# The feed-forward's last down products, moved into the first two steps of the attention that follows

## The chip, the cores and the metric

The kernel runs on one core of one Trainium2 chip. The metric is the device time of one execution in microseconds, the median over several runs. A profiled execution is a separate one; its durations are used to cost single steps, and its own total is given beside its span. The engines are named as in the profile: PE (TensorE matmuls), PEld (its weight loads), DVE (VectorE), ACT (ScalarE), POOL (GpSimd), SP (the engine that issues most DMAs).

## The reference

Input is x, 4096 tokens (16 sequences of 256) of 256 values, all in float32. Four parts follow one another, each with a residual sum and a layer norm:

```python
x = layernorm(x + L0_attn(x))   # a linear recurrence with decay, 16 heads of 128
x = layernorm(x + L0_ffn(x))    # silu(x Wg) * (x Wu) @ Wd, hidden size 704, weights stored as integers
x = layernorm(x + L1_attn(x))   # latent attention: 16 heads, causal, 256 keys per sequence
x = layernorm(x + L1_ffn(x))    # 32 experts, 4 per token, and two shared experts
```

The second one, `down(silu(gate) * up)`, and the third matter here. In the third, a token's query goes through a latent of 192 values and its keys and values through one of 64, each with an RMS norm:

```python
cq  = rms_norm(x @ w_qa.T)                  # 192
ckv = x @ w_kva.T                           # 64 latent + 64 rotary
q   = cq @ w_qb.T                           # 16 heads of 128 + 64 rotary
k, v = (rms_norm(ckv[:64]) @ w_kvb.T)       # per head 128 and 128
out = softmax(mask(q k.T * scale)) @ v @ w_o.T
```

The kernel does not form k and v: it multiplies w_qb with w_kvb's key half, and w_kvb's value half with w_o, once (the "products" below, tiles w_q, w_qr and w_ov), and then scores and sums over the 64-value latent itself.

## The kernel before

Tokens are taken in 8 blocks of 512 (`NB`), each of four tiles of 128 tokens (`NTT`); x lies in SBUF throughout (`xs`, of which `x_t` are the tiles).

**The feed-forward** (from about 860 us) is a loop over blocks, `for b in range(NB)`. A block has five chunks of gate and up matmuls over 512 tokens (`glu`, line 211; silu on ACT, line 219; the product on DVE, line 221) and a half chunk (`glu_rest`, lines 229 to 243). Both write the gated values `hT`, from a pool with two buffers. Then comes the next block's transposed x (line 182), and then the previous block's down products: `finish_ffn(b, hT)` runs two pairs of token tiles (`down`, lines 250 and 256; ten matmuls of 128x256 and two of 64x256 in each pair) into two PSUM tiles `d_ps`, and `added` adds them to x on DVE (line 192) and takes the layer norm: statistics on DVE (153, 154), a scalar step on DVE (144), a power on POOL (145), the normalising step on DVE (169). After the loop the last block's `finish_ffn` is called once more; nothing else of the feed-forward is left then.

In blocks 2 and 3 the loop also runs `products(0)` and `products(1)`, each for eight heads (matmuls at 816 and 829, copies at 823 on DVE and 836 on ACT). Their weights come in two halves `wqb` and `wo1` in one buffer each (DMAs at 781 and 783), so that the second half waits for the last reader of the first; `wkvb` is loaded whole (762). Blocks 4 to 7 run the latents of the second attention's block 0 in pieces (`latents`).

**The second attention** (to about 1907 us) runs 64 steps of one pair of heads over one block, with an order written out by hand under `tc.manual_schedule`: each engine executes its instructions in the order of the code. The loop is `for n in range(-2, NS + 1)`. Step n does three things for different pairs: it asks for the queries of pair n + 2 (`queries`, PE lines 1075 and 1081, two PSUM tiles from a pool of three; `turn`, the rotary part, three DVE operations at 1090 to 1092 and an addition on POOL at 1093), scores pair n + 1 (`scores`, PE 1111, two PSUM buffers; `maxima`, DVE 1122; `exps`, ACT 1135; `divide`, a reciprocal on DVE at 1146 and a product on POOL at 1148), and forms the contexts of pair n - 1 (`keys_first`, transposes on PE 1161 and a copy `aT` on ACT 1165; `contexts`, PE 1174; the copy into `cT` on ACT 1336). Steps -2 and -1 have no contexts yet, and step 0 neither.

Between these come, piece by piece, the latents of the next block: `latents(1)` runs in the first steps. It has a transposed x, four latent tiles (PE 687, copy 694 and squares 697 on ACT), the RMS scale (DVE 144, POOL 145), eight scaled copies `cq` on ACT (711, 712), the key side `kf` on DVE (720 to 732), and transposes (739, 746). Three latent tiles are taken in step -2 and the fourth in step -1. In the code of one step the order is:

```python
heads[0].scores / maxima / exps         # pair n+1, first head
sms[n][1].divide()                      # second head of pair n
q_ps = queries(...)                     # pair n+2
heads[0].divide()
aTs0 = keys_first(pair, 0)              # pair n-1
qTs[asked] = [turn(...) ...]
heads[1].scores(...); contexts(...); keys_first(pair, 1)
heads[1].maxima(...); second_place(...) # latents, outputs, routing
heads[1].exps(...); contexts(...)
```

After it come the experts. Their weights `w_e` are loaded by 26 DMAs that SP issues from about 1870 us on, as their space, which the second attention's tiles hold, comes free; the first expert product is at 1993.44 us.

## Time and profile before

| | |
|---|---|
| time, median of 3 runs | 2123.05 us (2122.95 to 2123.97) |
| profiled execution | 2142.67 us, of which the span is 2140.9 us |
| mean granted TensorE clock in it | 0.991 |
| PE busy | 2056.8 us, 96% of the span |
| DVE, ACT, POOL busy | 1567.0 (73%), 754.8 (35%), 878.3 us (41%) |
| first attention | to about 860 us |
| feed-forward | about 860 to 1124 us |
| second attention | about 1112 to 1907 us |
| first expert product | 1993.44 us |

The profiled execution took 19.6 us more than the median of the runs; rows of the profile are read against its own total. A row of the timeline has the start in the span, the busy time, the engine, the line, the operation with its output and inputs, and in brackets the idle time of the engine just before it and what released it. The share of busy time is a mean over the four stages, so a stage is read by its own stretch.

### The profile page before, as it was taken

The page shows a single profiled execution, that of the slowest core. Times are in us where ns is not written, and L with a number is a line of the kernel's source. Part 1 is how long each engine was busy: PE and PEld are TensorE (multiplying, and loading weights), DVE is VectorE, ACT ScalarE, POOL GpSimd, SP SyncE. Part 2 cuts the span into 40 slices and gives each one's busy share as a digit, 9 for nine tenths or more (in the row PEclk, how much of TensorE's full clock was granted, in tenths as well). Part 3 has the DMA queues.
Part 4 walks back from the last instruction along what each step waited for, and adds up shares of the span by engine and source line. Part 5 has one row for each costly group of instructions (what it writes and reads, how often), then busy time and mean ns, then how long its engine had stood idle before and what let it go on. Part 6 is the DMA issues. An engine that isn't in the chain of part 4 may idle for free.

```text
span 2140.9 us, 29447 instructions
## 1 busy us (share of the span) xinstructions
PE 2056.8 (96%) x9496; PEld 1434.1 (67%) x9496; DVE 1567.0 (73%) x4000; ACT 754.8 (35%) x2213; POOL 878.3 (41%) x948
## 2 busy tenths in 40 slices
PE   8999999999999999999998999999999999988897
PEld 5777777777777777556565666666666666664675
DVE  7888888888888887232327669797988879873556
ACT  2212121212111211211315566656565665541233
POOL 5622232323232322000005554667575767653357
PEclk9999999999999999999999999999999999999999
DMA  9544444444444220300000000000000000050438
GB/s 310 188 133 148 133 140 133 138 128 138 134 143 121 90 89 29 90 16 20 1 1 1 1 1 1 24 9 6 3 4 2 3 3 3 10 186 2 137 131 321
DMA packets 101402, 169.73 MB, mean 79 GB/s; under 512 B 17527, under 2 KB 66431, under 8 KB 99072
## 3 DMA queue, kind: packets, MB, share of 16 engines
q1 hardware_dynamic: 88512, 158.45, 23.3%
q0 software_dynamic: 8064, 5.18, 0.8%
q10 hardware_dynamic: 4672, 4.21, 0.6%
q8 instruction: 76, 1.25, 0.2%
q14 instruction: 78, 0.64, 0.1%
HBM read 128.76 MB, written 56.95 MB: 87 GB/s over the span
## 4 chain that ended last, share of the span: by engine, by line
PE 75%; DVE 16%; ACT 3%; issue 3%; DMA 1%; POOL 1%; another core or an unknown queue 1%; POOLq 0%; DVEq 0%; SPq 0%; ACTq 0%
PE p_ps L422 16%; PE o_ps L515 10%; PE v_ps L452 9%; PE s_ps L1111 5%; PE g_ps L211 4%; PE u_ps L211 4%; PE o_ps L1193 4%; PE d_ps L250 3%; PE q_ps L1075 3%; PE c_ps L1174 3%; PE a_ps L1161 3%; DVE sm L1122 2%; PE q_ps L1081 2%; DVE turned L1092 2%; DVE turned L1091 1%
## 5 line engine op out<-in xcount | busy, mean ns | idle before, releaser
L502 POOL TENSOR_TENSOR wkv<-su,Wr_sb 128x512 f32<-128x512 f32 x128 | 160.2, 1273 | 503.2 <-PE p_ps L422 313.9
L1148 POOL TENSOR_TENSOR pr<-pr,rr 128x256 f32<-128x256 f32 (+1 forms) x256 | 206.9, 836 | 153.3 <-DVE rr L1146 126.0
L515 PE MATMUL o_ps<-w_o,wkv 128*128 128x256 f32 (+1 forms) x1024 | 251.6, 388 | 6.1 <-POOL wkv L502 5.8
L1135 ACT ACTIVATE pr<-sm,nm 128x128 f32<-128x128 f32 (+1 forms) x512 | 226.2, 444 | 78.9 <-DVE nm L1122 64.7
L452 PE MATMUL v_ps<-xm,w_Wv 128*128 128x512 f32 x512 | 242.4, 596 | 6.5 <-DMA w_Wv<-in_Wv_dram 6.5
L515 PEld LDWEIGHTS o_ps<-w_o,wkv 128*128 128x128 f32 x1024 | 192.1, 190 | 75.7 <-POOL wkv L502 44.9
L1111 PE MATMUL s_ps<-kT,qT 128*128 128x128 f32 (+1 forms) x1024 | 198.0, 337 | 23.6 <-DVE nm L1122 23.6
L424 ACT COPY t_sb<-p_ps 128x256 f32<-128x256 f32 x128 | 47.4, 370 | 467.1 <-PE p_ps L422 465.7
L422 PE MATMUL p_ps<-xm,w_Wk 128*128 128x256 f32 x896 | 204.3, 379 | 1.5 <-DVE Wr_sb L427 1.5
L422 PEld LDWEIGHTS p_ps<-xm,w_Wk 128*128 128x128 f32 x896 | 170.4, 190 | 52.7 <-issue 27.8
L422 PE MATMUL p_ps<-xm,w_Wr 128*128 128x256 f32 x896 | 204.4, 379 | 0.7 <-POOL xm L404 0.5
L1093 POOL TENSOR_TENSOR qT<-qT,turned 128x512 f32<-128x512 f32 x128 | 162.8, 1274 | 87.7 <-DVE turned L1092 86.5
L422 PEld LDWEIGHTS p_ps<-xm,w_Wr 128*128 128x128 f32 x896 | 170.0, 190 | 25.2 <-DVE Wk_sb L427 0.9
L1111 PEld LDWEIGHTS s_ps<-kT,qT 128*128 128x128 f32 x1024 | 146.0, 193 | 44.5 <-issue 36.9
L1165 ACT COPY aT<-a_ps 128x384 f32<-128x384 f32 x256 | 109.9, 480 | 167.3 <-PE a_ps L1161 167.2
L473 DVE TENSOR_TENSOR_SCAN st<-decay,kv 128x255 f32<-128x255 f32 x256 | 163.8, 681 | 4.4
L1122 DVE CUSTOM_DVE_ANT_0 sm<-s_ps,const 128x128 f32<-128x128 f32 (+1 forms) x512 | 154.1, 353 | 14.5 <-PE s_ps L1111 11.5
L1007 POOL DMA_INDIRECT xp_d<-xs,dest x128 | 128.3, 1003 | 59.5 <-issue 30.9
L497 ACT ACTIVATE Wr_sb<-Wr_sb 128x512 f32<-128x512 f32 x128 | 73.5, 621 | 217.7 <-DVE Wr_sb L430 188.7
L145 POOL TENSOR_TENSOR rstd<-rs_t,nhalf 128x4 f32<-128x4 f32 (+1 forms) x33 | 33.3, 1010 | 285.0 <-DVE rs_t L144 274.5
L452 PEld LDWEIGHTS v_ps<-xm,w_Wv 128*128 128x128 f32 x512 | 97.7, 191 | 74.8 <-issue 61.8
L221 DVE TENSOR_TENSOR hT<-sg,u_ps 128x512 f32<-128x512 f32 x56 | 38.4, 686 | 139.7 <-PE u_ps L211 131.4
(190 smaller groups left out, 3711.4 us busy)
## 6 DMA issues: line engine op xcount, KB each, us to landing
w_Wk<-wsum_d SPq DMA_DIRECT2D x56, 448.0 KB
w_Wr<-wsum_d SPq DMA_DIRECT2D x56, 448.0 KB
w_Wv<-in_Wv_dram SPq DMA_DIRECT2D x64, 256.0 KB
res_d<-zeros SPq DMA_DIRECT2D x16, 1024.0 KB
res<-res_d SPq DMA_DIRECT2D x16, 1024.0 KB
w_e<-in_W_experts_dram SPq DMA_DIRECT2D x32, 384.0 KB
xp_d<-empty SPq DMA_DIRECT2D x4, 1360.0 KB
xe<-xp_d SPq DMA_DIRECT2D x32, 136.0 KB
```

The source lines that it names most:

```text
L211: mm = nc.tensor.matmul(ps, lhsT=w[:, c, i * P : (i + 1) * P], rhs=xT[:, c, :], start=(c == 0), stop=(c == DC - 1),)
L422: nc.tensor.matmul(to, lhsT=w[:, at, :], rhs=x[:, bt, :], start=True, stop=True)
L452: nc.tensor.matmul(ps, lhsT=self.w3["Wv"][:, 2 * h + c, :], rhs=self.xms["Wv"][:, 2 * c : 2 * c + 2, :].rearrange("p s t -> p (s t)"), sta ...
L473: nc.vector.tensor_tensor_scan(st[:, s, 1:], decay[:, n : n + 1].to_broadcast([P, S - 1]), kv[:, s, : S - 1], 0.0, ALU.mult, ALU.add,)
L502: nc.gpsimd.tensor_tensor(wkv, self.su[h], self.both(self.r, h), ALU.mult)
L515: nc.tensor.matmul(ps.rearrange("p t d -> p (t d)") if opens else ps[:, tt % 2, :], lhsT=self.wkv[h][:, tt * P : (tt + 1) * P], rhs=w_o[:, ...
L1007: put = nc.gpsimd.indirect_dma_start(out=xp_d[:, :], out_offset=bass.IndirectOffsetOnAxis(ap=dest[:, k, t : t + 1], axis=0), in_=xs[b][:, ...
L1093: nc.gpsimd.tensor_tensor(qT, qT, qr, ALU.add)
L1111: nc.tensor.matmul(ps[:, lo:hi], lhsT=qT[:, s * S + i * P : s * S + (i + 1) * P], rhs=kT[:, s * S : s * S + hi - lo], start=True, stop=True,)
L1122: nc.vector.tensor_tensor_reduce(out=sm[:, lo:hi], in0=self.ps[s][:, lo:hi], in1=cst["mask"][:, lo:hi], scale=-(DQ**-0.5), scalar=-MASKED, ...
L1135: nc.scalar.activation(self.pr[:, s, lo:hi], self.sm[s][:, lo:hi], AF.Exp, bias=self.nm[:, s, i : i + 1], scale=-1.0, accum_out=self.rs[:, ...
L1148: nc.gpsimd.tensor_tensor(self.pr[:, :, lo:hi], self.pr[:, :, lo:hi], rr[:, :, i : i + 1].to_broadcast([P, 2, hi - lo]), ALU.mult,)
```

## The change

The last block's down products leave the end of the feed-forward. Their two pairs become a generator, `downs`; the attention's loop takes one pair in step -1 and one in step 0, just after the queries. Their PSUM tiles stand, until step 1, in the two banks that later hold the transposed probabilities. The adds to x stand in step 0 and the layer norm in step 2.

For this, the last block's gated values and w_down have to live on into the attention. The gated values of odd blocks are written into `ctx_h`, the space of the contexts `cT`, which has two buffers as before; even blocks have a buffer of their own. w_down gets a pool `wd` apart from the other weights, closed at step 1, and the copies `aT` then get a pool that opens at step 1. To make room, the weights for the products come in quarters (`wqb`, `wo1` and now also `wkvb`, four heads each) and `products(0)` to `products(3)` run in blocks 1 to 4.

```diff
-    def glu(xT, wg, wu, chunks, pool, psum, tag, more=0):
-        hT = pool.tile([P, chunks + more, BLK], F32, tag="hT", name="hT")
+    def glu(xT, wg, wu, chunks, pool, psum, tag, hT=None):
+        if hT is None:
+            hT = pool.tile([P, chunks, BLK], F32, tag="hT", name="hT")
...
+    pc = att.enter_context(tc.tile_pool(name="ctx", bufs=1, reuse_waits="tile"))
+    ctx_h = pc.tile([P, 2, NH // 4, BLK], F32, name="ctx_h")
...
+    def load_quarter(part):
+        rows = slice(part * QH * P, (part + 1) * QH * P)
+        wqb = wt.tile([P, QH, QLR], F32, tag="wqb", name="wqb")
+        nc.sync.dma_start(out=wqb, in_=a["w_qb_nope"][rows, :].rearrange("(h p) j -> p h j", p=P))
+        wo1 = wt.tile([P, QH, D], F32, tag="wo1", name="wo1")
+        nc.sync.dma_start(out=wo1, in_=a["w_o"][rows, :].rearrange("(h p) d -> p h d", p=P))
+        wkvb = wt.tile([P, QH, 2, KVLR], F32, tag="wkvb", name="wkvb")
+        rows = slice(2 * rows.start, 2 * rows.stop)
         nc.sync.dma_start(
+            out=wkvb, in_=a["w_kvb"][rows, :].rearrange("(h x p) c -> p h x c", x=2, p=P)
         )
+        return wqb, wo1, wkvb
+    quarters = [load_quarter(part) for part in range(4)]
+    def down_pairs(two, hT):
+        os = []
+        for pair in range(NTT // 2):
+            pss = [ps[:, pair, :] for ps in two]
+            down(pss, hT, w_down, 2 * pair)
+            os += pss
+            yield os
...
+        hT2 = [
+            ph_.tile([P, NF + 1, BLK], F32, name="hT", bufs=1),
+            ctx_h.rearrange("p i j t -> p (i j) t")[:, : NF + 1, :],
+        ]
...
+            hT = glu(xT, w_gate, w_up, NF, ph_, ps_g, "g", hT2[b % 2])
...
-                if b in (NB - 6, NB - 5):
-                    products(b - NB + 6)
-            finish_ffn(*last)
+            if NB - 7 <= b <= NB - 4:
+                products(b - NB + 7)
...
+        psd = ExitStack()
+        ps_d = psd.enter_context(tc.tile_pool(name="ps_d2", bufs=2, space=PSUM))
+        two = [ps_d.tile([P, 2, D], F32, tag="d", name="d_ps") for _ in range(2)]
+        downs = down_pairs(two, last[1])
...
+                if n == 1:
+                    psd.close()
+                    ffd.close()
+                    ps_a = ph.enter_context(tc.tile_pool(name="ps_a", bufs=2, space=PSUM))
+                    ps_c = ph.enter_context(tc.tile_pool(name="ps_c", bufs=1, space=PSUM))
+                    pt = ph.enter_context(tc.tile_pool(name="att_t", bufs=4))
...
+                if n in (-1, 0):
+                    os = next(downs)
                 if scored is not None:
                     heads[0].divide()
...
-                        cT = cTs[seen // NP, part] = pc.tile(
-                            [P, NP // 2, BLK], F32, tag="cT", name="cT"
-                        )
+                        cT = cTs[seen // NP, part] = ctx_h[:, part]
...
+                if n == 0:
+                    x = x_t[(NB - 1) * NTT :]
+                    for o, y in zip(os, x):
+                        nc.vector.tensor_tensor(y, o, y, ALU.add)
+                if n == 2:
+                    layernorm(x_t[(NB - 1) * NTT :], x_t[(NB - 1) * NTT :])
```

More of the change, by code (lines that the diff above doesn't have):

```diff
@@ L193, in added @@
         layernorm(x, x)
-    ffw = ExitStack()
+    ffd, ffw = ExitStack(), ExitStack()
+    wd = ffd.enter_context(tc.tile_pool(name="wd", bufs=1, side="right"))
+    w_down = wd.tile([P, NF + 1, D], F32, name="w_down")
     wf = ffw.enter_context(tc.tile_pool(name="wf", bufs=1, side="right"))
@@ L200, in seq_postln_kernel @@
     w_gu = wf.tile([P, DC, 2 * HALF], F32, name="w_gu")
-    w_down = wf.tile([P, NF + 1, D], F32, name="w_down")
-    def glu(xT, wg, wu, chunks, pool, psum, tag, more=0):
-        hT = pool.tile([P, chunks + more, BLK], F32, tag="hT", name="hT")
+    def glu(xT, wg, wu, chunks, pool, psum, tag, hT=None):
+        if hT is None:
+            hT = pool.tile([P, chunks, BLK], F32, tag="hT", name="hT")
         for i in range(chunks):
@@ L749, in latents @@
         yield
-    with ExitStack() as ph:
-        wt = ph.enter_context(tc.tile_pool(name="wt", bufs=1, reuse_waits="tile"))
+    pc = att.enter_context(tc.tile_pool(name="ctx", bufs=1, reuse_waits="tile"))
+    ctx_h = pc.tile([P, 2, NH // 4, BLK], F32, name="ctx_h")
+    wts = ExitStack()
+    wt = wts.enter_context(tc.tile_pool(name="wt", bufs=1, reuse_waits="tile"))
+    nc.sync.dma_start(
+        out=w_lat[:, :, :QLR], in_=a["w_qa"].rearrange("(c p) o -> p c o", p=P)
+    )
+    nc.sync.dma_start(
+        out=w_lat[:, :, QLR:], in_=a["w_kva"].rearrange("(c p) o -> p c o", p=P)
+    )
@@ new lines, in seq_postln_kernel @@
+    nc.sync.dma_start(out=q_ln, in_=a["q_a_ln_w"])
+    nc.sync.dma_start(out=kv_ln, in_=a["kv_a_ln_w"].partition_broadcast(P))
+    w_pe = a["w_qb_pe"].rearrange("p (h k d) -> p h k d", k=2, d=DR)
+    nc.sync.dma_start(
+        out=w_q[:, :, KVLR:], in_=a["w_qb_pe"][:P, :].rearrange("p (h d) -> p h d", h=NH)
+    )
+    for k in range(2):
+        nc.sync.dma_start(out=w_qr[k * QR : (k + 1) * QR, :, KVLR:], in_=w_pe[P:, :, k, :])
+    nc.sync.dma_start(
+        out=w_router, in_=a["router_w"].rearrange("(c p) e -> p c e", p=P)
+    )
@@ new lines, in seq_postln_kernel @@
+    nc.sync.dma_start(out=e_bias, in_=a["e_bias"].partition_broadcast(P))
+    for w, n in ((sh_gate, "shared_gate"), (sh_up, "shared_up"), (sh_down, "shared_down")):
+        nc.sync.dma_start(out=w, in_=a[n].rearrange("(c p) o -> p c o", p=P))
+    QH = NH // 4
+    def load_quarter(part):
[6 more added lines that the diff above has]
+        rows = slice(2 * rows.start, 2 * rows.stop)
@@ L753, in seq_postln_kernel @@
         nc.sync.dma_start(
-            out=w_lat[:, :, :QLR], in_=a["w_qa"].rearrange("(c p) o -> p c o", p=P)
+            out=wkvb, in_=a["w_kvb"][rows, :].rearrange("(h x p) c -> p h x c", x=2, p=P)
         )
-        nc.sync.dma_start(
-            out=w_lat[:, :, QLR:], in_=a["w_kva"].rearrange("(c p) o -> p c o", p=P)
-        )
-        nc.sync.dma_start(out=q_ln, in_=a["q_a_ln_w"])
-        nc.sync.dma_start(out=kv_ln, in_=a["kv_a_ln_w"].partition_broadcast(P))
-        wkvb = wt.tile([P, NH, 2, KVLR], F32, name="wkvb")
@@ L762, in seq_postln_kernel @@
-        nc.sync.dma_start(
-            out=wkvb, in_=a["w_kvb"].rearrange("(h x p) c -> p h x c", x=2, p=P)
-        )
-        w_pe = a["w_qb_pe"].rearrange("p (h k d) -> p h k d", k=2, d=DR)
-        nc.sync.dma_start(
-            out=w_q[:, :, KVLR:], in_=a["w_qb_pe"][:P, :].rearrange("p (h d) -> p h d", h=NH)
-        )
-        for k in range(2):
-            nc.sync.dma_start(out=w_qr[k * QR : (k + 1) * QR, :, KVLR:], in_=w_pe[P:, :, k, :])
-        nc.sync.dma_start(
-            out=w_router, in_=a["router_w"].rearrange("(c p) e -> p c e", p=P)
-        )
@@ L774, in seq_postln_kernel @@
-        nc.sync.dma_start(out=e_bias, in_=a["e_bias"].partition_broadcast(P))
-        for w, n in ((sh_gate, "shared_gate"), (sh_up, "shared_up"), (sh_down, "shared_down")):
-            nc.sync.dma_start(out=w, in_=a[n].rearrange("(c p) o -> p c o", p=P))
-        halves = []
-        for h in (0, NH // 2):
-            rows = slice(h * P, (h + NH // 2) * P)
-            wqb = wt.tile([P, NH // 2, QLR], F32, tag="wqb", name="wqb")
-            nc.sync.dma_start(out=wqb, in_=a["w_qb_nope"][rows, :].rearrange("(h p) j -> p h j", p=P))
-            wo1 = wt.tile([P, NH // 2, D], F32, tag="wo1", name="wo1")
-            nc.sync.dma_start(out=wo1, in_=a["w_o"][rows, :].rearrange("(h p) d -> p h d", p=P))
-            halves.append((wqb, wo1))
@@ L787, in seq_postln_kernel @@
-        with ExitStack() as ff:
-            ph_ = ff.enter_context(tc.tile_pool(name="h1", bufs=2, reuse_waits="tile"))
-            ps_t = ff.enter_context(tc.tile_pool(name="ps_t", bufs=2, space=PSUM))
-            ps_g = ff.enter_context(tc.tile_pool(name="ps_g", bufs=4, space=PSUM))
-            ps_d = ff.enter_context(tc.tile_pool(name="ps_d", bufs=2, space=PSUM))
-            def finish_ffn(b, hT):
-                os = []
-                two = [ps_d.tile([P, 2, D], F32, tag="d", name="d_ps") for _ in range(2)]
-                for pair in range(NTT // 2):
-                    pss = [ps[:, pair, :] for ps in two]
-                    down(pss, hT, w_down, 2 * pair)
-                    os += pss
-                added(b, os)
-            def products(part):
-                wqb, wo1 = halves[part]
-                pairs = range(part * NH // 4, (part + 1) * NH // 4)
-                for pair in pairs:
-                    ps3 = ps_t.tile([P, BLK], F32, tag="t", name="wq_ps")[:, : 3 * KVLR].rearrange(
-                        "p (k d) -> p k d", k=3
-                    )
-                    ps, ps_r = ps3[:, :2, :], ps3[:, 2, :]
-                    for k in range(2):
-                        h = 2 * pair + k
-                        for to, lo, n in ((ps[:, k, :], 0, P), (ps_r[k * QR : (k + 1) * QR, :], P, QR)):
-                            nc.tensor.matmul(
-                                to,
-                                lhsT=wqb[:, h - part * NH // 2, lo : lo + n],
-                                rhs=wkvb[:, h, 0, :],
-                                start=True,
-                                stop=True,
-                            )
-                    nc.vector.tensor_copy(w_q[:, 2 * pair : 2 * pair + 2, :KVLR], ps)
-                    nc.vector.tensor_copy(w_qr[:, pair, :KVLR], ps_r)
-                for pair in pairs:
-                    ps = ps_t.tile([P, BLK], F32, tag="t", name="wo_ps")[:, :D]
-                    for k in range(2):
-                        h = 2 * pair + k
@@ new lines, in load_quarter, with finish_ffn, products @@
+        return wqb, wo1, wkvb
[7 more added lines that the diff above has]
+            yield os
+    with ExitStack() as ff:
+        ph_ = ff.enter_context(tc.tile_pool(name="h1", bufs=2, reuse_waits="tile", side="right"))
+        hT2 = [
+            ph_.tile([P, NF + 1, BLK], F32, name="hT", bufs=1),
+            ctx_h.rearrange("p i j t -> p (i j) t")[:, : NF + 1, :],
+        ]
+        ps_t = ff.enter_context(tc.tile_pool(name="ps_t", bufs=2, space=PSUM))
+        ps_g = ff.enter_context(tc.tile_pool(name="ps_g", bufs=4, space=PSUM))
+        ps_d = ff.enter_context(tc.tile_pool(name="ps_d", bufs=2, space=PSUM))
+        def finish_ffn(b, hT):
+            two = [ps_d.tile([P, 2, D], F32, tag="d", name="d_ps") for _ in range(2)]
+            for os in down_pairs(two, hT):
+                pass
+            added(b, os)
+        def products(part):
+            wqb, wo1, wkvb = quarters[part]
+            pairs = range(part * QH // 2, (part + 1) * QH // 2)
+            for pair in pairs:
+                ps3 = ps_t.tile([P, BLK], F32, tag="t", name="wq_ps")[:, : 3 * KVLR].rearrange(
+                    "p (k d) -> p k d", k=3
+                )
+                ps, ps_r = ps3[:, :2, :], ps3[:, 2, :]
+                for k in range(2):
+                    h = 2 * pair + k
+                    for to, lo, n in ((ps[:, k, :], 0, P), (ps_r[k * QR : (k + 1) * QR, :], P, QR)):
@@ L829, in products @@
                         nc.tensor.matmul(
-                            ps[k * KVLR : (k + 1) * KVLR, :],
-                            lhsT=wkvb[:, h, 1, :],
-                            rhs=wo1[:, h - part * NH // 2, :],
+                            to,
+                            lhsT=wqb[:, h - part * QH, lo : lo + n],
+                            rhs=wkvb[:, h - part * QH, 0, :],
                             start=True,
@@ L835, in products @@
                         )
-                    nc.scalar.copy(w_ov[:, pair, :], ps)
-            last = None
-            xT = transposed(0, mo_x, ps_t, "t")
-            for b in range(NB):
-                hT = glu(xT, w_gate, w_up, NF, ph_, ps_g, "g", 1)
-                glu_rest(xT, hT, ph_, ps_g, "g")
-                with tc.issue_after(last_of["ACT"]):
-                    for _ in ends[0]:
-                        pass
-                if b + 1 < NB:
-                    xT = transposed(b + 1, mo_x, ps_t, "t")
-                if last is not None:
-                    finish_ffn(*last)
-                last = (b, hT)
-                if b in (NB - 6, NB - 5):
-                    products(b - NB + 6)
-                if b == NB - 4:
-                    first_latents = latents(0, ps_t, "t")
-                if b >= NB - 4:
-                    for _ in range(3):
-                        next(first_latents, None)
@@ L858, in seq_postln_kernel @@
-            finish_ffn(*last)
-        ffw.close()
+                nc.vector.tensor_copy(w_q[:, 2 * pair : 2 * pair + 2, :KVLR], ps)
+                nc.vector.tensor_copy(w_qr[:, pair, :KVLR], ps_r)
+            for pair in pairs:
+                ps = ps_t.tile([P, BLK], F32, tag="t", name="wo_ps")[:, :D]
+                for k in range(2):
+                    h = 2 * pair + k
+                    nc.tensor.matmul(
+                        ps[k * KVLR : (k + 1) * KVLR, :],
+                        lhsT=wkvb[:, h - part * QH, 1, :],
+                        rhs=wo1[:, h - part * QH, :],
+                        start=True,
+                        stop=True,
+                    )
+                nc.scalar.copy(w_ov[:, pair, :], ps)
@@ new lines, in seq_postln_kernel @@
+        last = None
+        xT = transposed(0, mo_x, ps_t, "t")
+        for b in range(NB):
+            hT = glu(xT, w_gate, w_up, NF, ph_, ps_g, "g", hT2[b % 2])
+            glu_rest(xT, hT, ph_, ps_g, "g")
+            with tc.issue_after(last_of["ACT"]):
+                for _ in ends[0]:
+                    pass
+            if b + 1 < NB:
+                xT = transposed(b + 1, mo_x, ps_t, "t")
+            if last is not None:
+                finish_ffn(*last)
+            last = (b, hT)
+            if NB - 7 <= b <= NB - 4:
+                products(b - NB + 7)
+                if b == NB - 4:
+                    wts.close()
+            if b == NB - 4:
+                first_latents = latents(0, ps_t, "t")
+            if b >= NB - 4:
+                for _ in range(3):
+                    next(first_latents, None)
@@ L862, in seq_postln_kernel @@
+    ffw.close()
     GT = NTT
@@ L1055, in seq_postln_kernel @@
         pa = ph.enter_context(tc.tile_pool(name="att", bufs=4))
-        pc = ph.enter_context(tc.tile_pool(name="ctx", bufs=2))
         ps_m = ph.enter_context(tc.tile_pool(name="ps_m", bufs=3, space=PSUM))
         ps_s = ph.enter_context(tc.tile_pool(name="ps_s", bufs=2, space=PSUM))
-        ps_a = ph.enter_context(tc.tile_pool(name="ps_a", bufs=2, space=PSUM))
-        ps_c = ph.enter_context(tc.tile_pool(name="ps_c", bufs=1, space=PSUM))
+        psd = ExitStack()
+        ps_d = psd.enter_context(tc.tile_pool(name="ps_d2", bufs=2, space=PSUM))
+        two = [ps_d.tile([P, 2, D], F32, tag="d", name="d_ps") for _ in range(2)]
+        downs = down_pairs(two, last[1])
         NP = NH // 2
@@ L1163, in keys_first @@
                     )
-                aT = pa.tile([P, 3 * P], F32, tag="aT", name="aT")
+                aT = pt.tile([P, 3 * P], F32, tag="aT", name="aT")
                 copy = nc.scalar.copy(aT, a_ps)
@@ L1305, in seq_postln_kernel @@
                     if j == 0:
-                        cT = cTs[seen // NP, part] = pc.tile(
-                            [P, NP // 2, BLK], F32, tag="cT", name="cT"
-                        )
+                        cT = cTs[seen // NP, part] = ctx_h[:, part]
                     c_ps = ps_c.tile([P, 2, S], F32, tag="c", name="c_ps")
```

## The prediction

> **What bounds the kernel.** The page's table of engines came first: PE is busy for 2056.8 of 2140.9 us. So an edit pays only where PE stands still, and the next question is whether it stands still where this change works. I asked for busy time by stretch (columns: length, PE, PEld, DVE, ACT, POOL busy, granted PE clock, DMA share, GB/s).

> ```profile
> PE 2056.8 (96%) x9496; PEld 1434.1 (67%) x9496; DVE 1567.0 (73%) x4000; ACT 754.8 (35%) x2213; POOL 878.3 (41%) x948
> ...
> 860.00:1111.00 251.00, 251.00 (x876) 143.31 (x876) 69.20 (x197) 52.58 (x108) 10.57 (x12) 1.00 0.10 24
> 1130.00:1150.00 20.00, 14.91 (x55) 8.69 (x53) 13.20 (x46) 12.26 (x48) 12.24 (x13) 0.91 0.00 1
> 1150.00:1162.00 12.00, 8.71 (x34) 5.60 (x36) 9.34 (x34) 4.58 (x18) 5.86 (x7) 0.72 0.00 1
> 1186.00:1198.00 12.00, 11.32 (x61) 6.22 (x61) 7.50 (x29) 7.43 (x29) 7.68 (x9) 1.00 0.01 2
> 875.00:880.00 5.00, 5.00 (x17) 2.52 (x16) 0.69 (x1) 2.09 (x5) 0.00 (x0) 1.00 0.77 239
> 880.00:885.00 5.00, 5.00 (x16) 2.85 (x15) 1.54 (x3) 1.64 (x4) 0.00 (x0) 1.00 0.00 0
> ```

> The feed-forward (860 to 1111) has PE full: nothing moved inside it gains, and nothing costs that keeps PE fed. The start of the second attention (1130 to 1162) has PE idle for 8.4 of 32 us, at a clock of 0.91 and 0.72; its steady state (1186 to 1198) is at 94% and full clock. The timeline says what the start waits for:

> ```profile
> 1106.29 4.58 PE L250 MATMUL d_ps<-w_down,hT 128*128 128x256 f32 x20
> 1110.80 0.70 PE L256 MATMUL d_ps<-w_down,hT 64*128 64x256 f32 x4
> ...
> 1134.97 1.58 PE L1111 MATMUL s_ps<-kT,qT 128*128 128x128 f32 x8
> ...
> 1136.38 1.24 PE L687 MATMUL lat_ps<-w_lat,xT 128*128 128x320 f32 x4
> ...
> 1140.47 2.90 PE L1111 MATMUL s_ps<-kT,qT 128*128 128x128 f32 x8 [2.85 <-DVE nm L1122]
> ...
> 1142.15 0.40 ACT L711 ACTIVATE cq<-lat,rms 128x128 f32<-128x128 f32 x1 [3.19 <-POOL rms L145]
> ...
> 1148.13 0.18 DVE L1146 RECIPROCAL rr<-rs 128x4 f32<-128x4 f32 x1 [1.57 <-ACT pr L1135]
> ...
> 1153.29 2.90 PE L1111 MATMUL s_ps<-kT,qT 128*128 128x128 f32 x8 [5.47 <-DVE nm L1122]
> ```

> Two scores wait for a maximum on DVE (3.0 us of PE idle before 1140.47, 5.6 before 1153.29). The second ends a chain: last latent tile (1136.38), its copy and squares on ACT, rms on POOL, eight cq on ACT, exponentials, reciprocal on DVE (1148.13), two turns, maximum (1152.50), score. After each wait the scores take 2.90 us where 1.58 is usual: half clock.

> **The removed term.** A down pair is PE from 1106.28 to 1111.43, 5.15 us; block 7's two are 10.3 us. They stand between block 7's last gated values and the first latents (1112.8 to 1124.23, one q product in between). The compiled order puts them, in after, behind the queries of step -1 and of step 0. So I walked the rows' durations forward in that order: queries 2.87 (L1075 and L1081), two scores 1.30, latent tile 1.07, pair 5.15; on DVE a head's turn 2.13, a maximum 0.56, reciprocal 0.18; on ACT exponentials 0.89 a score, table load 1.28, a latent's copy and squares 1.38, cq 2.35; POOL's add 1.27, divide 1.6. The same walk in the old order meets the trace within about 0.3 us, the slow clock apart (a score pair at half clock is 1.3 longer).

> **Start to step 0.** Queries of pair 0 start at 1112.26. The second latent tile waits 1.26 for a buffer, held until the first turn; before, the downs covered that turn. Scores at 1119.6 (before 1130.69), queries of pair 1 at 1120.9 (before 1132.10): 11.2 earlier. That is 0.9 over 10.3, because the layer norm of block 7 (add 1.42, statistics 1.40 and 0.36 to 0.39, normalising 1.38) no longer stands ahead of the turns.

> **Pair one, step -1 (1123.77 to 1128.92).** It hides the turns of pair 1, but stands ahead of the last latent tile: 1130.2, only 6.2 earlier than 1136.38. The wait of 3.0 us is gone: scores at 1131.3, queries of pair 2 at 1132.6, 10.6 earlier than 1143.16.

> **Pair two, step 0 (1135.46 to 1140.61).** It lies wholly under the ACT chain. From the last latent tile to the second waiting score the chain took 16.9 us before (1136.38 to 1153.29); 1.65 of this, the squares' scalar step (L144) queued behind turns and maxima on DVE, goes, since DVE is ahead now. So that score comes at 1130.2 + 15.3 = 1145.5, 7.8 earlier, and PE still idles 3.6 us (1141.9 to 1145.5) where it idled 5.6.

> **What comes back.** Queries of pair 3 start at 1146.8 against 1155.98, 9.2 earlier: 7.8 and the 1.4 that half clock cost there. Step 0 also has the adds on DVE (four, 1.42), and the first contexts wait 1.1 us for ACT's copy: queries of pair 4 at 1158.2 against 1166.29, 8.1 earlier, and the next pair's the same, 8.0. At step 2 DVE has the layer norm: statistics 1.40 and 0.36, a scalar step 0.17, a wait of 1.2 for POOL's power (1.02, behind two adds of 1.27), normalising 1.38: 4.5 us. Queued behind it on DVE is the reciprocal, then the turns; PE waits for those. The steady step has about 0.8 us of PE idle in 9.55 and DVE 6.9 busy, so part of the 4.5 is absorbed: 2.7 comes through. From there on every step is as before, 5.4 earlier. Bounds of these two give-backs: zero (DVE's 2.7 spare us a step hide both) and 5.9 (nothing hidden, 4.5 + 1.4); the walk's 3.8 lies between.

> **The clock.** The 3.6 us of idle left in after may bring half clock again. The 3.0 us before 1140.47 was enough. [...] So the gain is 5.4 (clock holds) or 4.1 (it doesn't); I take the middle, 4.7, as the time is a median over executions.
> [...]

> **The products in quarters.** The same matmuls and copies, in blocks 1 to 4 rather than 2 and 3: cost 0, hidden by nothing but PE's own full row, since they move within it. What is new is waiting for loads. The first set lands by 880 (239 GB/s, then 0) and is first used at about 911, after block 0's downs. Three reloads follow (wqb 384 KB, wo 512, wkvb 256, each waiting for the previous quarter's last reader). A block is 251/8 = 31.4 us, and a half's reload of twice the size landed within some 5 us of its issue:

> ```profile
> SPq L781 <- PE wq_ps L816: 77.2, 1, 77.2
> ...
> SPq L783 <- PE wo_ps L829: 16.1, 1, 16.1
> ```

> On SP these waits already stand; behind them are only other reloads and, from 1870 on, the expert weights. SP gets seven more issues (0.4 to 1.1 us each), off the path. Bounds: 0, and what a landing above some 25 us would leave over, three times; I take 0.

> **The shared space.** Contexts keep their two buffers. aT lies in w_down's space, first written at step 1, after both pairs. Expert loads from about the sixth on lie over the contexts and wait for the last output (1907) rather than for issues between 1898 and 1916: at most some 15 us later, with the first expert product at 1993.44, so hidden. If that cover were gone, each us beyond 1993 would show in full.

> **Sum.** The profiled execution is 2142.67 (span 2140.9 and 1.8 outside), less 4.7 is 2138.0. It is 19.6 above the median of 2123.05; carrying the difference over, 2123.05 - 4.7 = 2118.35, say 2118.3. A measurement of this kernel tells about 0.2%, 4.25 us, from no change, so the line is 2118.8, close by.

> **Rivals.**
> (a) *The start is one chain, and what is put into it lengthens it.* Pair one delays the last latent tile by its full 5.15, pair two delays the score that the chain releases, by 5.15 too, and the layer norm and adds come back as 3.8: 2123.05 - 10.3 + 10.3 + 3.8 = 2126.9, slower. For: pair one does stand ahead of the last latent. Against: ACT's wait of 3.19 for rms and the idle after 1147.8 are not PE's. It decides at 1140.6: if the chain's score is ready before pair two ends, pair two is uncovered. 0.15, slips in loads included.
> (b) *Little gain.* Cover is as worked but the layer norm and adds come through whole (5.9, not 3.8) with half clock: 5.4 - 2.1 - 1.3 = 2.0, so 2121.0; no measurable change. 0.15.
> (c) *Full cover.* DVE's spare time hides the step-2 norm: 5.4 + 2.7 = 8.1, so 2115.0. For: DVE is busy 7.5 of 12 us in steady state. Against: its turn is what the scores wait for. 0.08.
> (d) *No move.* The scheduler might put the pairs back; the compiled order shows them at steps -1 and 0, and their last adds and norm at 0 and 2. Under 0.01.

> **How the numbers follow.** Forecast 0.62, between 2117.7 and 2118.9 by the clock, widened by the walk's 0.3 a side and more for its length: 2117 to 2119.7. Of it some 0.42 lies below 2118.8, 0.20 above. Faster 0.42 + 0.08 = 0.50; within 0.2% 0.20 + 0.15 = 0.35; slower 0.15. The range takes in (b) and (c) and leaves out (a): 2115.0 to 2123.0.

> **What would show it.** Right: a feed-forward as full as before up to xT_ps at about 1111.4; d_ps rows in two pieces of 5.15 near 1124 and 1135; first scores near 1119.6; one wait of about 3.6 us for nm in place of two; in steady state the queries 5 us earlier than before; a longer step at n = 2. Wrong: PE idle before a wq_ps with a DMA as releaser; a wait over 5 us before the same score; a stall over 4 us at step 2; expert products later than their 1993.44 less the gain.

## The result, and the profile after

The changed kernel took 2117.39 us in the median of 13 runs (2115.46 to 2120.94), beside 2123.42 us for the kernel before in 13 runs on the same chip: a ratio of 0.997, 95% interval 0.9962 to 0.9977. That is 6.0 us less by the medians and 4.9 to 8.1 us less by the interval; the forecast was 4.7 less, 2118.3, in a range of 2115.0 to 2123.0. The profiled execution took 2116.8 us with a span of 2115.0 us.

The stretches of the timeline, in the columns of the prediction, for the changed kernel:

```profile
860.00:1111.00 251.00, 251.00 (x875) 143.20 (x873) 69.03 (x198) 52.60 (x108) 10.47 (x12) 1.00 0.09 24
...
1130.00:1150.00 20.00, 17.31 (x77) 11.17 (x76) 12.50 (x53) 9.65 (x40) 8.26 (x9) 1.00 0.00 1
1150.00:1162.00 12.00, 10.80 (x70) 7.38 (x68) 8.54 (x30) 8.81 (x31) 8.83 (x10) 1.00 0.01 1
1186.00:1198.00 12.00, 11.32 (x67) 7.74 (x66) 9.16 (x34) 7.61 (x28) 7.28 (x8) 1.00 0.01 2
875.00:880.00 5.00, 5.00 (x17) 2.67 (x16) 0.69 (x1) 1.88 (x5) 0.00 (x0) 1.00 0.02 3
```

The feed-forward is as full as before, 251.00 of 251 us, and the first, smaller set of the products' weights has landed by 875. At the attention's start (1130 to 1162) PE idles for 3.9 us where it idled for 8.4, and the granted clock is 1.00 throughout. The steady state has not changed.

PE's rows of the changed kernel in the same place:

```profile
1117.77 2.42 PE L689 MATMUL lat_ps<-w_lat,xT 128*128 128x320 f32 x8 [0.92 <-DVE turned L1115]
...
1124.20 4.58 PE L252 MATMUL d_ps<-w_down,ctx_h 128*128 128x256 f32 x20
1128.72 0.70 PE L258 MATMUL d_ps<-w_down,ctx_h 64*128 64x256 f32 x4
1129.35 1.58 PE L1134 MATMUL s_ps<-kT,qT 128*128 128x128 f32 x8
1130.76 1.24 PE L689 MATMUL lat_ps<-w_lat,xT 128*128 128x320 f32 x4
...
1136.02 4.58 PE L252 MATMUL d_ps<-w_down,ctx_h 128*128 128x256 f32 x20
1140.53 0.70 PE L258 MATMUL d_ps<-w_down,ctx_h 64*128 64x256 f32 x4
1141.16 1.58 PE L1134 MATMUL s_ps<-kT,qT 128*128 128x128 f32 x8
1145.43 1.55 PE L1134 MATMUL s_ps<-kT,qT 128*128 128x128 f32 x8 [2.69 <-DVE nm L1145]
```

One pair stands ahead of the fourth latent tile (1130.76), the other just behind the queries of step 0. Of the two long waits for a maximum one is left, of 2.69 us, and the scores behind it run at their usual 1.55 us. The layer norm is among the last DVE work of step 2, so it is step 3 that waits, four times:

```profile
1171.84 1.55 PE L1134 MATMUL s_ps<-kT,qT 128*128 128x128 f32 x8 [0.74 <-DVE nm L1145]
1174.09 0.87 PE L1197 MATMUL c_ps<-aT,kf 128*64 128x256 f32 x8 [0.70 <-ACT aT L1188]
...
1176.44 0.87 PE L1197 MATMUL c_ps<-aT,kf 128*64 128x256 f32 x8 [0.68 <-ACT aT L1188]
1178.46 1.55 PE L1134 MATMUL s_ps<-kT,qT 128*128 128x128 f32 x8 [1.15 <-DVE nm L1145]
```

In the kernel before, this step has one such wait, of 0.68 us for aT; the others are new. From that step's queries (1167.36, pair 5) to the next ones (1179.84, pair 6) it takes 12.48 us instead of 9.55.

### The profile page after: what moved, and what is told of

Same layout as the page of the kernel before. It is cut to its first block, busy times and chain, and to the rows that moved or that the text cites. A ratio compares the mean times of both kernels' runs of the same rounds, so it can differ in the third digit from the quotient of the medians.

```text
span 2115.0 us, 29449 instructions
## 1 busy us (share of the span) xinstructions
PE 2045.0 (97%) x9496; PEld 1427.6 (67%) x9496; DVE 1568.5 (74%) x4000; ACT 756.2 (36%) x2213; POOL 878.7 (42%) x948
## 4 chain that ended last, share of the span: by engine, by line
PE 73%; DVE 16%; issue 4%; ACT 3%; POOL 2%; DMA 1%; SPq 0%; POOLq 0%; DVEq 0%; ACTq 0%
PE p_ps L424 16%; PE o_ps L517 10%; PE v_ps L454 9%; PE s_ps L1134 5%; PE o_ps L1216 4%; PE g_ps L213 4%; PE u_ps L213 4%; PE q_ps L1098 3%; PE d_ps L252 3%; PE a_ps L1184 3%; PE c_ps L1197 3%; PE q_ps L1104 2%; DVE sm L1145 2%; PE gu_ps L1546 1%; DVE turned L1115 1%
## 5 line engine op out<-in xcount | busy, mean ns | idle before, releaser
L1145 DVE CUSTOM_DVE_ANT_0 sm<-s_ps,const 128x128 f32<-128x128 f32 (+1 forms) x512 | 153.9, 354 | 13.0 <-PE s_ps L1134 10.6
L145 POOL TENSOR_TENSOR rstd<-rs_t,nhalf 128x4 f32<-128x4 f32 (+1 forms) x33 | 33.2, 1006 | 302.4 <-DVE rs_t L144 301.9
L1197 PE MATMUL c_ps<-aT,kf 128*64 128x256 f32 (+1 forms) x1024 | 111.5, 339 | 12.7 <-ACT aT L1188 12.7
```

The lines of the kernel that those rows point to most:

```text
L1145: nc.vector.tensor_tensor_reduce(out=sm[:, lo:hi], in0=self.ps[s][:, lo:hi], in1=cst["mask"][:, lo:hi], scale=-(DQ**-0.5), scalar=-MASKED, ...
L1197: mm = nc.tensor.matmul(c_ps[k * KVLR : (k + 1) * KVLR, s, i * P :], lhsT=kf[:, 2 * s + i, :KVLR], rhs=aT[:, : 2 * P] if i == 0 else aT[:, ...
```

## The experiments

All profiles are compared by the distance between two PE rows, since the feed-forward's end lies up to 1.7 us apart in different executions: from the first queries to the last output products of the attention (the group of 32 matmuls). e1 to e4 ran on one chip and e5 to e8 on another; the kernel before had a median of 2124.55 us (16 runs) on the first and 2124.23 (21 runs) on the second, so medians of the two can be set side by side to about 0.3 us.

| kernel | time, median us (runs) | ratio to before, 95% | first queries to last outputs, us |
|---|---|---|---|
| before, profiled anew (e5) | 2122.97 (1) | | 787.8 |
| layout alone (e1) | 2123.71 (11) | 0.9997 (0.9988 to 1.0006) | 787.7 |
| the change (first comparison) | 2117.39 (13) | 0.9970 (0.9962 to 0.9977) | 782.0 |
| the change again (e2) | 2116.77 (6) | 0.9973 (0.9961 to 0.9985) | 782.7 |
| latent tile first (e3) | 2113.83 (5) | 0.9950 (0.9936 to 0.9964) | 779.5 |
| norm in step 5 (e4) | 2116.63 (5) | 0.9964 (0.9950 to 0.9978) | 780.9 |
| both pairs in step -1 (e6) | 2124.12 (11) | 0.9999 (0.9990 to 1.0008) | 788.2 |
| both pairs in step 0 (e7) | 2120.96 (11) | 0.9986 (0.9977 to 0.9995) | 786.5 |
| latent tile first, norm spread (e8) | 2111.15 (5) | 0.9937 (0.9924 to 0.9951) | 776.8 |

**e1, the layout without the move.** Quarters, shared space and pools of the changed kernel; the last block's downs stay in the feed-forward.

```diff
+        finish_ffn(*last)
...
-        two = [ps_d.tile([P, 2, D], F32, tag="d", name="d_ps") for _ in range(2)]
-        downs = down_pairs(two, last[1])
...
-                if n in (-1, 0):
-                    os = next(downs)
```

The call stands just behind the loop over blocks; the adds of step 0 and the layer norm of step 2 are gone with it.

> The quarters of weights, the contexts' shared space and the pools as in the changed kernel, but the last block's two down pairs, adds and layer norm stay at the end of the feed-forward as before. Theory 1 (all of the gain is the two pairs lying under waits of the second attention's start): equal to before within 1 us, 2122.4 to 2124.4; in the trace two waits of the scores for nm (3 and 5.6 us) as before. Theory 2 (the quarters or the changed order of the feed-forward bring part of the gain): 2119 to 2121. Theory 3 (the layout costs something that the move hides): above 2125.

Time and trace are those of before: ratio 0.9997, 787.7 us, and the two waits and the half-clock scores behind them, at a granted clock of 0.91 in 1130 to 1150 and 0.83 in 1150 to 1170, stand where they stood:

```profile
1140.32 2.90 PE L1133 MATMUL s_ps<-kT,qT 128*128 128x128 f32 x8 [2.85 <-DVE nm L1144]
1153.14 2.90 PE L1133 MATMUL s_ps<-kT,qT 128*128 128x128 f32 x8 [5.54 <-DVE nm L1144]
```

So the quarters, their extra loads and the reordered feed-forward neither give nor cost anything that shows; all of the gain is the move. Theories 2 and 3 fall.

**e2, the change again**, unedited.

> The changed kernel once more, as the measure for the variants beside it. Both theories: 2117.4 with a spread of some 3 us; pair two ends at about 1141 us in the trace and the score released by nm starts near 1145.4. If the clock after that wait is what spreads its times, its granted clock in 1140 to 1160 varies from one profile to the next.

2116.77 us, and the same rows up to the wait of 2.69 us. This time the granted clock fell behind it (0.91 in 1130 to 1150):

```profile
1144.76 1.63 PE L1134 MATMUL s_ps<-kT,qT 128*128 128x128 f32 x8 [2.69 <-DVE nm L1145]
1146.18 3.54 PE L1098 MATMUL q_ps<-cqT,w_q 128*128 128x512 f32 x4
...
1156.11 1.58 PE L1134 MATMUL s_ps<-kT,qT 128*128 128x128 f32 x8
```

The queries took 3.54 instead of 1.88 us. But the queries of pair 4 start 45.55 us behind the first ones, against 45.18 in the first profile of this kernel: of 1.7 us only 0.4 came through, since in the first profile PE waited there anyway (1.02 us before the scores that stand last in the fence, 0.17 before the contexts), and here it does not. So this event does not explain the 7 us by which this kernel's times spread in these runs (2115.21 to 2122.62); where the slower ones lose theirs stays open. The mean granted clock of an execution doesn't tell: it is 0.995 in the slowest of the first comparison (2120.94 us), but 0.996 both in the slowest here (2122.62) and in the profiled one (2115.27).

**e3, the fourth latent tile ahead of pair one.**

```diff
-                if n in (-1, 0):
+                if n == 0:
                     os = next(downs)
...
                 elif n == -1:
-                    for _ in range(2):
-                        step_latents(1)
+                    step_latents(1)
+                    os = next(downs)
+                    step_latents(1)
```

> In step -1 the fourth latent tile goes ahead of pair one of the downs (pair one behind the second head's scores and that tile, not ahead of them); pair two stays in step 0. Theory 1 (pair one costs what it delays the chain latent, rms, cq, exponentials by, 5.15 us, of which 3.6 shows as PE idle): the idle before the score that waits for nm falls from 2.9 to below 1 us; 2.0 to 2.8 us less than the changed kernel, about 2114.9. Theory 2 (the remaining wait is set by DVE and ACT work that doesn't depend on that tile): no gain, the same wait at the same place.

2113.83 us, 2.9 less than the change (e2) on the same chip; its trace and the change's first one differ by 2.4 us at pair 9's queries and 2.5 at the last outputs. The wait is gone:

```profile
1143.88 1.55 PE L1134 MATMUL s_ps<-kT,qT 128*128 128x128 f32 x8 [0.17 <-DVE nm L1145]
```

Theory 1 holds: what was left of that wait was pair one standing ahead of the tile that feeds the chain.

**e4, the layer norm in step 5.** `if n == 2:` becomes `if n == 5:` ahead of `layernorm`.

> The last block's layer norm stands in step 5 instead of step 2; step 5 has output products of 3.6 us on PE more. Theory 1 (DVE's 4.5 us of layer norm push the turns of step 2 and cost 2.7 us of PE there, and in step 5 they lie beside the outputs): 2.0 to 2.7 us less than the changed kernel, about 2115; step 2 takes 9.55 us instead of 12.5. Theory 2 (the cost follows the norm wherever it stands): step 2 shorter, step 5 longer by as much, same time.

Both theories are half right. Step 3, behind the old place, takes 9.55 us again, 2.93 less, and step 6, behind the new one, takes 13.65 instead of 12.26: 1.39 come back, with waits for nm and aT at another place.

```profile
1202.89 1.55 PE L1134 MATMUL s_ps<-kT,qT 128*128 128x128 f32 x8 [0.39 <-DVE nm L1145]
1205.14 0.87 PE L1197 MATMUL c_ps<-aT,kf 128*64 128x256 f32 x8 [0.70 <-ACT aT L1188]
```

Against the change's first trace the net is 1.5 us there and 1.0 at the last outputs; the medians differ by 0.1 us, which five and six runs with spreads of 4.5 and 7.4 us do not resolve.

**e5, the kernel before again.**

> The kernel before once more, for a profile whose stages after the attention can be set beside the changed kernel's. If the 19.6 us by which the first profiled execution lay over its median belong to that execution alone, this one takes about 2123, the time from its last output products (L1193 near 1900) to the end is about 220 us, as in the changed kernel, and the two waits for nm at the attention's start and the half clock behind them are as in the first one.

2122.97 us, span 2121.1. From its last outputs (1900.40) to the end it takes 220.7 us, as the changed kernel does (220.4); the first profiled execution took 240.7. So the 19.6 us were that execution's own, behind the attention, and carrying the difference over was right. The two waits are the first profile's:

```profile
1140.66 2.90 PE L1111 MATMUL s_ps<-kT,qT 128*128 128x128 f32 x8 [2.84 <-DVE nm L1122]
1153.48 2.90 PE L1111 MATMUL s_ps<-kT,qT 128*128 128x128 f32 x8 [5.47 <-DVE nm L1122]
```

Set beside this profile the change's gain is 6.1 us of span, 5.9 of it between the first queries and the last outputs.

**e6, both pairs in step -1.** `if n in (-1, 0): os = next(downs)` becomes `if n == -1:` with a loop over all of `downs`.

> Both down pairs in step -1, ahead of the fourth latent tile, none in step 0. Theory 1 (the wait at the end of the start is a chain from that tile, so a pair ahead of it adds its full 5.15 us and a pair behind it is free): 5.15 us more than the changed kernel, about 2122, and the wait for nm in step 0 grows from 2.7 to about 7.8 us. Theory 2 (any of the free places in the start takes a pair): same as the changed kernel, 2117.

2124.12 us, no gain at all over before (ratio 0.9999), and 2 us above what theory 1 had; theory 2 falls. The wait grew as theory 1 foresaw, and half clock, which it did not count, came with it (the granted clock is 0.87 in 1150 to 1170, where the change has 1.00):

```profile
1151.13 2.90 PE L1134 MATMUL s_ps<-kT,qT 128*128 128x128 f32 x8 [7.83 <-DVE nm L1145]
1153.83 2.54 PE L1098 MATMUL q_ps<-cqT,w_q 128*128 128x512 f32 x4
```

The wait is 5.14 us longer than in the change, just one pair; 1.3 us of the scores and 0.7 of the queries at half clock come on top, and 6.2 us are left at the last outputs, since later waits take up a part.

**e7, both pairs in step 0.** The same with `if n == 0:`.

> Both down pairs in step 0, none in step -1. Theory 1 (the tile is 5.15 us earlier and step 0 covers both pairs, but step -1's scores of the next pair then wait for the maxima behind the turns on DVE, some 3.6 us of PE idle): within 0.5 us of the changed kernel, about 2117, the PE wait moved from before the second score of step 0 to before the first. Theory 2 (only the chain from that tile counts): 2.5 to 3.6 us less, about 2114.

2120.96 us: 4 more than the change (e2), where one theory had the same time and the other a gain, so both missed. The wait did move to the first scores, 3.13 us, as theory 1 had it, but the clock fell behind it (0.98 in 1111 to 1130, 0.93 in 1130 to 1150), and again in step 3, behind the layer norm (0.94 in 1170 to 1200; the change has 1.00 in all three):

```profile
1129.29 2.89 PE L1134 MATMUL s_ps<-kT,qT 128*128 128x128 f32 x8 [3.13 <-DVE nm L1145]
1131.97 2.26 PE L1098 MATMUL q_ps<-cqT,w_q 128*128 128x512 f32 x4
...
1180.38 2.80 PE L1134 MATMUL s_ps<-kT,qT 128*128 128x128 f32 x8 [1.14 <-DVE nm L1145]
1182.98 2.35 PE L1098 MATMUL q_ps<-cqT,w_q 128*128 128x512 f32 x4
```

Each time the scores take 1.3 us longer and the queries 0.4 to 0.5. Two times 1.7 is 3.4 of the 4.5 us by which the last outputs are later than in the change. In step 3 the rows show the 1.7 in full: 1.2 more than in the change at pair 6's queries, 1.7 at pair 7's. For the first event it is argued: the waits behind it, 0.17, 0.28 and 1.01 us up to pair 4's queries, are as long as in e3, which has no half clock (0.17, 0.28 and 1.02, at a granted clock of 1.00 in 1111 to 1200), so they have taken up nothing. PE's waits up to pair 3's queries are also 0.6 us longer than in the change (3.13 and 0.17 against 2.69).

**e8, the fourth latent tile first and the norm spread.** On top of e3:

```diff
-                if n == 2:
-                    layernorm(x_t[(NB - 1) * NTT :], x_t[(NB - 1) * NTT :])
+                if n in (1, 2):
+                    for i in (2 * n - 2, 2 * n - 1): ...   # bn_stats, bn_aggr of tile i
+                if n == 2:
+                    rsqrt(rstd7, mv7[:, :, 1], 1.0, LN_EPS)
+                if n in (3, 4):
+                    for i in (2 * n - 6, 2 * n - 5): ...   # normalise tile i
```

> As e3 (the fourth latent tile ahead of pair one), and the last block's layer norm spread over steps 1 to 4: statistics of two tiles in each of steps 1 and 2, the power at the end of step 2, two normalising operations in each of steps 3 and 4. Theory 1 (DVE has some 2.7 us to spare in a step, so pieces of about 1 us are hidden where 4.5 us at once cost 2.9): 2 to 2.9 us less than e3, about 2111.5; step 2 takes 9.6 us. Theory 2 (each piece delays the turns that PE waits for): step by step the pieces come back, 2113 to 2114.

2111.15 us (2109.66 to 2111.69), 2.7 less than e3 and 5.6 less than e2 by the medians, 5.2 less than the change at the last outputs, and a ratio of 0.9937 to the kernel before: the best of all that ran. The waits of PE between 1111 and 1200, by what it waited for (total, times, longest), in the kernel before (e5), the change and e8:

```profile
PE s_ps L1111 <- DVE nm L1122: 8.3, 2, 5.5
```

```profile
PE s_ps L1134 <- DVE nm L1145: 5.6, 4, 2.7
```

```profile
PE s_ps L1134 <- DVE nm L1145: 1.2, 2, 1.0
```

Steps 2, 3 and 4 take 9.55 us each, so pieces of about 1 us (in the change's rows two tiles' statistics take 1.1 us and two normalising operations 0.7) are hidden where the whole norm cost 2.9. The edit does one thing more: DVE, which in the change stood 1.13 us in the norm waiting for POOL's power, has other work meanwhile. How much of the gain is this, and how much the size of the pieces, is not separated.

## Why the prediction was right, and where its sizes were off

The time lies in the range, on the side that was forecast, for the reason that was given. The walk, as starts of the queries counted from the first ones, beside the traces:

| queries of pair | before (e5) | walk | after | what stands between |
|---|---|---|---|---|
| 1 | 19.74 | 8.64 | 8.70 | downs no longer ahead |
| 2 | 30.80 | 20.34 | 20.52 | pair one |
| 3 | 43.61 | 34.54 | 34.19 | pair two, the wait for nm |
| 4 | 53.92 | 45.94 | 45.18 | adds, first contexts |
| 6 | 73.03 | 67.74 | 67.21 | layer norm in step 2 |

**The removed term, pair one and pair two: right.** Down rows stand at 1124.20 and 1136.02 (walk 1123.8 and 1135.5), in 5.15 us each; the early wait is gone; the second score pair starts at 1145.43 (walk 1145.5). The wait ahead of it was sized too large, at 3.6 us, and measured 2.69: from the fourth latent tile to that score it took 14.67 us where the walk had 15.3, and pair two ended a little later than walked. That pair one costs what it delays the chain by, as far as PE stands idle for it, and pair two nothing, is shown by e6 (pair two ahead of the tile too: a wait 5.14 us longer) and e3 (no pair ahead of it: the wait gone, 2.4 us).

**What comes back: the adds and contexts too large, the norm a little too small.** The first contexts were to wait 1.1 us for ACT and waited 0.17; PE stood instead for a maximum, a few rows later:

```profile
1152.05 0.87 PE L1197 MATMUL c_ps<-aT,kf 128*64 128x256 f32 x8 [0.17 <-ACT aT L1188]
...
1156.42 1.55 PE L1134 MATMUL s_ps<-kT,qT 128*128 128x128 f32 x8 [1.02 <-DVE nm L1145]
```

Pair 4's queries came 0.8 us earlier than walked, pair 3's 0.35. The norm of step 2 was to cost 2.7 and cost 2.93. It shows in step 3, where the prediction looked for it in step 2; and what stands first behind it on DVE is the maxima (1171.05), not the reciprocal and the turns. Both together were put at 3.8 and measured 3.6: 9.4 less than before at pair 3's queries, 5.8 at pair 6's.

**The clock: the term that was mis-sized.** The forecast took 0.7 us off for half clock, the middle between none and 1.3 us, by which a score pair took longer in the kernel before (2.90 against 1.58 us). That about half of the executions would lose it was the author's estimate; no run shows such a share. That half clock comes and goes in the same place is right: of the three profiles with that wait of 2.69 us (the change's two and e4) one has it. But in that one, e2, it costs 0.4 us up to pair 4's queries, since the waits that follow take it up. Counted as in the table, the walk without a clock term gives 5.3 us at pair 6's queries and the trace 5.8; the middle between "holds" and "doesn't" took the 0.7 us off, where 0.2 (half of 0.4) would have been the size. That rests on one profile, and at the last outputs the two differ by 0.8.
So the gain was forecast 1.3 us too small by the medians, some 0.7 of it by the clock and 0.5 by the walk. The time itself came nearer, to 0.9, by luck: the kernel before measured 0.4 more in the comparison than in the three runs that the forecast started from, and the walk's errors (the wait too long, the norm too short) partly cancel.

**The products in quarters and the shared space: right, cost 0.** e1 measures them alone at a ratio of 0.9997. In the changed kernel the reloads were issued at 913 to 923, 947 to 957 and 981 to 991, by then with no PE gap in the whole stretch. The expert loads end well ahead of their use. By stretch, in the changed kernel:

```profile
1910.00:1930.00 20.00, 20.00 (x75) 12.46 (x75) 16.45 (x49) 6.21 (x10) 12.94 (x13) 0.91 0.82 303
1930.00:1950.00 20.00, 20.00 (x70) 11.84 (x69) 9.29 (x25) 3.46 (x6) 5.84 (x6) 1.00 0.01 2
```

They are done by 1930, and the first expert product, at about 1969, is earlier than in e5 (1974.51) by 5.5 us, most of the 5.8 by which the last outputs are earlier (1894.60 against 1900.40).

**The rivals.** (a), the start as one chain that every pair lengthens, is true of a pair ahead of the fourth latent tile, and e6 shows the place and the price; it is not true of pair two, which ended at 1141.16 with the chain's score at 1145.43. (b), little gain, fell: the adds and the norm gave back 3.6 us, not 5.9, and the clock cost 0.4, not 1.3. (c), full cover by DVE's spare time, is not what a norm in one piece gets (it costs 2.93 in step 2 and 1.39 in step 5), but it is what a norm spread over four steps gets (e8). (d) fell with the rows.

## What to carry to other kernels

PE work that is moved into a start-up's idle time was free here where it stood behind the instruction that feeds the chain the idle time waits for: pair two cost nothing there, and made the wait 5.14 us longer a step earlier (e6). But look at every idle place. With both pairs behind that instruction in step 0 (e7), step -1 was left uncovered and PE waited there; one pair in each step, each behind it (e3), was better. A lump of vector work longer than a pipelined step's spare time came through in part: the norm held DVE for 4.9 us (1166.20 to 1171.05), with 2.7 to spare in a steady step (6.9 busy of 9.55), and cost PE 2.9. So cut it into pieces shorter than the spare time before looking for a better step. Price a clock drop by whether the waits behind it take it up, not by the slow instructions alone.
